# First mixture of experts: results scattered with addition into one zeroed array instead of copied into two

## Chip, cores and metric

One core of one Trainium2 chip runs the whole kernel. The metric is the device time in microseconds (us) of one execution. The other seven cores are not used.

## What is computed

The reference is a graph network with two layers on 6250 nodes of width 256 and 100000 edges. Each layer is an attention step over the graph followed by a mixture of experts, and each of the four steps is added to its own input x. Cut to what matters here, the first mixture is

```python
rh = relu(features @ router_w1 + router_b1)
top_w, top_i = top_k(softmax(rh @ router_w2 + router_b2), 2)
weights = softmax(top_w)
# three layers for each of 6 experts, width 256
out = sum over the two chosen experts e of weights[e] * expert_e(features)
x = x + out
```

and what follows it is the second layer's projection, `h = layernorm(x) @ W` with two attention scores for each node, from which the second attention gathers rows by edge.

So every node gets exactly two rows of results from the first mixture, from two different experts, and the second projection needs x plus both.

## The kernel before

Nodes are laid out in 49 tiles of 128 rows. x itself stays in on-chip memory as `x_all`. The kernel is written in stages, and inside each stage the order of the work on each engine is written out by hand (`manual_schedule`).

**ffn0** is the first mixture with the first attention woven in. Its loop runs once per pair of tiles and then on until everything has drained. One turn of the loop does, for different pairs, blocks and groups at once: gather neighbours' rows (`takes0`, on POOL's queue), mix them into x, normalise, score the experts, choose two, and give every chosen row a slot in the region of its expert. `scatters` (L768, tile `f_rows`) then writes the rows to their slots in memory, with one indirect DMA for each tile and choice. A full region gives a *block* of 256 rows of one expert. `fetch` reads a block back (`xr`, on SP's queue, with that expert's weights `w`), and PE runs the three layers (L1038 and L1048). `drawn` scales the result on ACT (`by`, L892), and `finish` adds the bias on DVE (L897). There are 54 blocks.

Each block's result goes out in two halves of 128 rows with `send`, an indirect DMA on POOL's queue (L903, tile `f_parts`), 108 of them in all. The target `parts` has two halves, one for first choices and one for second choices, so that no row is written twice. `places` works out the row for each result (`btok`, six buffers; DVE L878 to L880). All these writes are declared independent of each other, so none waits for another. Up to two blocks are done per turn, so up to four sends are queued per turn.

POOL's queue also carries the two gathers for each tile, the scatters, and 49 small writes (`meta_d`, L232) that belong to the later sorting of nodes by degree. A round-robin deals these lists onto the queue. Where two of a kind would follow each other, a tiny `gap` memset is put between:

```python
lists = [steps, results, dispatch[:k], extra]
while any(lists):
    for k, x in enumerate(lists):
        if x:
            ...
            x.pop(0)()
```

After the loop, `sources` puts 49 gathers of edge lists (`idx`, L253) on POOL's queue.

**gnn1** is the second projection. `load` brings four tiles of each half of `parts` at a time on SP's queue (tile `yg`, L1186). `begin` adds both to `x_all` on DVE (L1203, two additions for each pair of tiles). `projected` then runs a software pipeline over 25 pairs of tiles: moments on DVE (L397, L398), square root and normalisation on ACT (L478, L471), transposes on PE (L475), a copy on ACT (`xT`, L462), projection on PE (`proj`, L446), a copy on ACT (`hb`, L481), and two stores to the table `t_d` (L1211, L1212). When the table has landed, POOL starts the second attention's gathers (`own` L1229, `g` L1239).

Of the kernel before, what the change touches and what calls it, by code (L numbers as in the profile page):

```python
# [35 lines left out]
def gnn_moe_kernel(ctx: ExitStack, tc: tile.TileContext, a: dict, out: bass.AP):  # L36
# [587 lines left out]
    class Routed:  # L624
# [2 lines left out]

        def __init__(self, name, n_e, keep_pool, ids, own=False, spare=None):  # L630
            self.name, self.n_e, self.ids, self.own = name, n_e, ids, own
            self.n_blocks = (2 * N + n_e * (NB - 1)) // NB
            self.spare = spare
            self.planned = self.n_blocks if spare is None else (2 * N + spare) // NB
            self.null_row = n_e * REG

            self.round = 0
            self.written_by = []
            self.part = NT * P + self.n_blocks * NB
            self.parts = dram.tile([2 * self.part, D], F32, name=f"{name}_parts")  # L640
            self.table = dram.tile([n_e * REG + NB, RW], F32, name=f"{name}_rows")
            self.kp = kp = keep_pool
            rank = kp.tile([P, n_e], F32, name="rank")
            nc.gpsimd.iota(rank, pattern=[[-1, n_e]], base=n_e, channel_multiplier=0,
                           allow_small_or_imprecise_dtypes=True)
            reg = kp.tile([P, n_e], F32, name="reg")
            nc.gpsimd.iota(reg, pattern=[[REG, n_e]], base=0, channel_multiplier=0,
                           allow_small_or_imprecise_dtypes=True)
            eid = kp.tile([P, n_e], F32, name="eid")
            nc.gpsimd.iota(eid, pattern=[[1, n_e]], base=0, channel_multiplier=0,  # L650
                           allow_small_or_imprecise_dtypes=True)
            valid = kp.tile([P, 1], F32, name="valid")
# [214 lines left out]
        def places(self, pool, xr, bcol, j, tok=None):  # L867

            w = pool.tile([P, NTB], F32, name="bw", bufs=4)
            first = pool.tile([P, NTB], F32, name="bfirst", bufs=4)  # L870
            nc.vector.tensor_scalar(first, xr[:, :, C_E0], bcol[:, self.n_c : self.n_c + 1], None, op0=OP.is_equal)
            nc.vector.tensor_mul(w, xr[:, :, C_WD], first)
            nc.vector.tensor_add(w, w, xr[:, :, C_W1])
            if tok is None:
                tok = pool.tile([P, NTB], I32, name="btok", bufs=6)

            off = pool.tile([P, NTB], F32, name="boff", bufs=4)
            nc.vector.tensor_scalar(off, xr[:, :, C_TOK], float(NT * P), float(j * NB), op0=OP.is_ge, op1=OP.mult)  # L878
            nc.vector.tensor_add(off, off, xr[:, :, C_TOK])
            nc.vector.scalar_tensor_tensor(tok, first, float(self.part), off, op0=OP.mult, op1=OP.add)  # L880
            return w, tok, first

        def put(self, pool, b, i, py):


            y = self.drawn(pool, b, i, py)
            self.finish(b, i, y)
            return y, b["tok"][:, i : i + 1]

        def drawn(self, pool, b, i, py):  # L890
            y = pool.tile([P, D], F32, name="by", bufs=4 if self.own else 12)
# [7 lines left out]
                nc.vector.scalar_tensor_tensor(y, b["xr"][:, i, :D], b["first"][:, i : i + 1], y,  # L899
                                               op0=OP.mult, op1=OP.add)  # L900

        def send(self, y, tok):
            put = nc.gpsimd.indirect_dma_start(  # L903
                out=self.parts[:, :], out_offset=bass.IndirectOffsetOnAxis(ap=tok, axis=0),
                in_=y, in_offset=None,
            )
            self.apart(put, "parts")
            tc.add_to_no_dep_group(f"{self.name}parts", put.ins)

        def due(self, n_rows, last):  # L910

# [13 lines left out]
        def left(self, out_i):  # L925
# [5 lines left out]
            nc.vector.tensor_tensor(s[0:1, 1:2], s[0:1, 1:2], s[0:1, 0:1], OP.max)  # L931
            nc.vector.tensor_copy(out_i, s)


    def prepare0(fp, k):

# [10 lines left out]
        bcast_rows(bias_b, a["L1_gnn_bias"])  # L947
        k["we1"], ab1 = gat_load(k["g1w"], a["L1_gnn_W"], (a["L1_gnn_att_src"], a["L1_gnn_att_dst"]))
        yield None
        k["moe"] = moe = Routed("f0", NX, fp, w_row)  # L950
        yield None
        bc = fp.tile([P, NX, 4], F32, name="b12c")
        with tc.tile_pool(name="f0cp", bufs=1, space=PSUM) as psum:
# [8 lines left out]
    def ffn0(k0, t0_d, a0_d, late, order_pool):  # L962
        NX = a["L0_ffn_expert_w1"].shape[0]
        moe, rw1, rw2, rb1, rb2 = (k0[k] for k in ("moe", "rw1", "rw2", "rb1", "rb2"))
        with tc.tile_pool(name="f0g", bufs=1) as fp, tc.tile_pool(name="f0r", bufs=2) as rp, \
                tc.tile_pool(name="f0w", bufs=4) as wp, tc.tile_pool(name="f0h", bufs=2) as hp, \
                tc.tile_pool(name="g0b", bufs=2) as gp:
            with tc.tile_pool(name="f0p", bufs=2, space=PSUM) as psum:
# [102 lines left out]

                while s < len(pairs) or ready or coming or new or q1 or q2 or q3 or g1 or g2 or g3 or drawn \
                        or dispatch or late or metas:
                    cur, new = new, [fetch(*b) for b in ready[:2]]
                    ready = ready[2:]
                    for b, i, y in drawn:
                        moe.finish(b, i, y)
                        results.append(partial(moe.send, y, b["tok"][:, i : i + 1]))
                    drawn = []
                    chore()  # L1080
                    for b in cur:
# [54 lines left out]
                    k = 2 if done < moe.n_blocks else 6  # L1136
                    extra, metas = metas[:k], metas[k:]
                    k = 8
                    lists = [steps, results, dispatch[:k], extra]
                    dispatch = dispatch[k:]  # L1140
                    while any(lists):
                        for k, x in enumerate(lists):
                            if x:
                                if k == last_kind and k != 0:
                                    nc.gpsimd.memset(gap, 0.0)
                                x.pop(0)()
                                last_kind = k
                    results = []
                    if g2 is not None:
                        dispatch += moe.scatters(g2["n"], g2["rw"], g2["slot"], g2["last"])  # L1150
# [18 lines left out]
    def gnn1(moe0, we, bias_b):  # L1169
# [3 lines left out]
        with tc.tile_pool(name="g1", bufs=2) as pool, tc.tile_pool(name="g1p", bufs=2, space=PSUM) as psum:  # L1173
# [3 lines left out]
            def load():  # L1177
                if not loads:
                    return
                g, n = loads.pop(0)  # L1180
                for c in range(2):
                    y = pool.tile([P, 4, D], F32, name=f"yg{c}", bufs=4)
                    r = c * moe0.part + g * P
                    k = min(n, NFULL - g)
                    if k:
                        nc.sync.dma_start(y[:, :k, :], moe0.parts[r : r + k * P, :].rearrange("(t p) d -> p t d", p=P))  # L1186
                    if k < n:
                        nc.sync.dma_start(y[:NTAIL, k, :], moe0.parts[r + k * P : r + k * P + NTAIL, :])
                    ys[g, c] = y

            def begin(q):
                if q is None:
# [2 lines left out]
                o = g % 4  # L1195
                if o == 0:
                    load()
                for c in range(2):
                    y = ys[g - o, c]
                    k = min(n, NFULL - g)  # L1200
                    if k:
                        xs = x_all[:, g : g + k, :]
                        nc.vector.tensor_add(xs, xs, y[:, o : o + k, :])  # L1203
                    if k < n:
                        xs = x_all[:NTAIL, NFULL, :]
                        nc.vector.tensor_add(xs, xs, y[:NTAIL, o + k, :])

            def store(q, hb):
                g, n = q["g"], q["n"]
# [1 line left out]
                nc.sync.dma_start(tv[:, :, :CX], hb[:, :n, :])  # L1211
                nc.sync.dma_start(tv[:, :, CX:], x_all[:, g : g + n, :])  # L1212

            for _ in range(3):
                load()
            projected(pool, psum, we, begin, store, lambda: None, lambda: False)
        return tab
# [203 lines left out]
    def ffn1(tab, bias_b):  # L1421
        NX, _, HD = a["L1_ffn_W1"].shape
        NM = HD // P
        with tc.tile_pool(name="f1", bufs=1) as fp, tc.tile_pool(name="f1r", bufs=2) as rp, \
# [13 lines left out]
            with tc.tile_pool(name="f1p", bufs=2, space=PSUM) as psum:  # L1438
# [74 lines left out]
                def fetch_kept(j):  # L1513
                    y = hp.tile([P, NTB, D], F32, name="late", bufs=3)
                    nc.sync.dma_start(y, y_d[j * P : (j + 1) * P])
                    return [partial(moe.send, y[:, i, :], toks[:, j, i : i + 1]) for i in range(NTB)]

                gap = fp.tile([1, 1], F32, name="gap")
                s = 0
# [250 lines left out]
```

## Time and profile before

| | us |
|---|---|
| median of 3 runs | 2446.48 (2446.15 to 2448.04) |
| the profiled execution, its own time | 2447.71 |
| its span, first to last instruction | 2446.0 |
| PE busy, share of the span | 1848.9 (76%) |
| POOL busy | 1498.5 (61%) |
| DVE busy | 1222.0 (50%) |
| ACT busy | 943.2 (39%) |
| 108 sends of the first mixture (L903), busy on POOL | 105.5, 977 ns each |

By the trace, the first projection fills about the first 125 us, ffn0 runs to about 734 us, gnn1 from there to about 835 us, the second attention with the second mixture to about 2383 us, and the final sum and output to the end.

PE is TensorE, PEld its weight loads, DVE VectorE, ACT ScalarE, POOL GpSimd, and SP the engine that issues most direct DMAs. Issuing instructions on SP do not count as busy. In a timeline row the first number is the start in us, the second the duration, and the bracket at the end gives the idle time before it and what ended that. A "landing" is the time from an issue until its data are there.

### The profile page before, as it was taken

The numbers are of one execution on the slowest core, as the hardware profiler recorded it, in microseconds if no ns is written. First come the engines' busy times: TensorE is split into PE (matmuls) and PEld (weight loads), VectorE is DVE, ScalarE is ACT, GpSimd is POOL, SyncE is SP. The second block draws the span as 40 slices with busy tenths as digits, with TensorE's granted clock in tenths as the row PEclk, the third lists the DMA queues.
The fourth block names the chain that finished last, engine by engine and source line by source line (L and its number), as shares of the span: only waits on it lengthen the run. The fifth ranks groups of instructions, "written<-read, shape, count | busy, mean of one in ns | idle before, by whom it ended". The sixth has DMA issues, their size and how long they took to land.

```text
span 2446.0 us, 31094 instructions
## 1 busy us (share of the span) xinstructions
PE 1848.9 (76%) x8343; PEld 1545.0 (63%) x8344; DVE 1222.0 (50%) x4459; ACT 943.2 (39%) x1967; POOL 1498.5 (61%) x1778
## 2 busy tenths in 40 slices
PE   3834757887986455259699999999989797799990
PEld 2622546676774343247588888887778676588880
DVE  3658765653227545365555565655645454311112
ACT  2754445553445421014244444433433332334330
POOL 2556366767637377777777777777777774244420
PEclk8955778998998876679899999999999898899995
DMA  7513354768769644446667767676666665387748
GB/s 215 125 42 118 107 161 134 220 191 243 232 196 299 182 116 109 109 155 188 189 197 245 244 209 243 204 226 222 204 199 204 200 198 157 123 295 258 277 163 314
DMA packets 346251, 471.68 MB, mean 193 GB/s; under 512 B 70205, under 2 KB 283236, under 8 KB 346070
## 3 DMA queue, kind: packets, MB, share of 16 engines
q1 hardware_dynamic: 261868, 272.15, 35.6%
q0 software_dynamic: 72112, 186.44, 25.6%
q10 hardware_dynamic: 12090, 11.03, 1.3%
q8 instruction: 69, 1.13, 0.2%
q14 instruction: 112, 0.92, 0.1%
HBM read 374.44 MB, written 95.02 MB: 192 GB/s over the span
## 4 chain that ended last, share of the span: by engine, by line
PE 38%; POOL 16%; DMA 10%; issue 9%; DVE 7%; ACT 7%; SPq 1%; POOLq 0%; DVEq 0%; ACTq 0%
PE py L1481 10%; PE ph L1470 10%; POOL g L1239 10%; PE sums L1293 7%; PE ph L1038 5%; DMA g<-t_d,idx 4%; POOL f_rows L768 2%; PE py L1048 2%; POOL idx L253 2%; DMA yg<-f_parts 2%; DMA idx<-src_d,start_i 2%; DVE g L1284 1%; ACT L1474 1%; ACT L402 1%; POOL f_parts L903 1%
## 5 line engine op out<-in xcount | busy, mean ns | idle before, releaser
L1239 POOL DMA_INDIRECT g<-t_d,idx x813 | 776.7, 955 | 249.2 <-issue 229.5
L1470 PE MATMUL ph<-bxT,w 128*128 128x256 f32 x1728 | 411.7, 396 | 29.6 <-ACT hT L1474 29.6
L1470 PEld LDWEIGHTS ph<-bxT,w 128*128 128x128 f32 x1728 | 338.2, 199 | 90.5 <-ACT hT L1474 43.0
L1293 PE MATMUL sums<-g,ident 128*128 128x256 f32 x1626 | 386.5, 397 | 3.1 <-DVE g L1284 3.0
L1481 PE MATMUL py<-w,hT 128*128 128x256 f32 x1728 | 384.9, 381 | 0.3 <-DMA w<-in_L_ffn_W 0.3
L1293 PEld LDWEIGHTS sums<-g,ident 128*128 128x128 f32 x1626 | 323.1, 200 | 59.9 <-DVE g L1284 12.5
L1481 PEld LDWEIGHTS py<-w,hT 128*128 128x128 f32 x1728 | 328.3, 191 | 45.1 <-DMA w<-in_L_ffn_W 0.5
L768 POOL DMA_INDIRECT f_rows<-rw,slot x196 | 199.4, 1017 | 91.8 <-issue 45.9
L897 DVE SCALAR_TENSOR_TENSOR by<-ob,bw,by 128x256 f32<-128x256 f32 x216 | 98.0, 481 | 266.9 <-ACT by L892 266.9
L1474 ACT ACTIVATE hT<-ph,bcol 128x256 f32<-128x256 f32 x432 | 177.9, 472 | 137.5 <-PE ph L1470 132.2
L1284 DVE TENSOR_TENSOR g<-g,weights 128x2048 f32<-128x2048 f32 (+6 forms) x88 | 229.6, 2610 | 0.0
L903 POOL DMA_INDIRECT f_parts<-by,btok x108 | 105.5, 977 | 153.1 <-DVE by L897 105.3
L1263 ACT ACT_TABLE_LOAD x36 | 46.2, 1283 | 391.7 <-DVE lg L1262 268.3
L1550 PE MATMUL pT<-ident,xn 128*128 128x128 f32 x98 | 24.5, 341 | 184.8 <-DVE xn L1547 184.8
L892 ACT ACTIVATE by<-py,bw 128x256 f32<-128x256 f32 x216 | 92.5, 473 | 154.9 <-PE py L1481 121.8
L1041 ACT ACTIVATE h<-ph,bcol 128x256 f32<-128x256 f32 x216 | 90.7, 471 | 158.6 <-PE ph L1038 97.8
L903 POOL DMA_INDIRECT f_parts<-by,toks x44 | 42.3, 961 | 161.8 <-DVE by L899 123.2
L1550 PEld LDWEIGHTS pT<-ident,xn 128*128 128x128 f32 x98 | 13.4, 167 | 197.5 <-issue 188.7
L1254 DVE TENSOR_TENSOR lg<-g,own 128x32 f32<-128x32 f32 (+6 forms) x88 | 16.7, 199 | 238.3 <-DMA g<-t_d,idx 211.2
L446 PE MATMUL proj<-we,xT 128*128 128x264 f32 x392 | 107.7, 421 | 27.5 <-ACT xT L462 27.5
L1038 PE MATMUL ph<-bxT,w 128*128 128x256 f32 x432 | 110.6, 412 | 16.0 <-ACT bxT L864 14.9
L1038 PE MATMUL ph<-h,w 128*128 128x256 f32 x432 | 112.8, 420 | 0.6 <-ACT h L1041 0.6
(325 smaller groups left out, 2909.7 us busy)
## 6 DMA issues: line engine op xcount, KB each, us to landing
w<-in_L_ffn_W SPq DMA_DIRECT2D x108, 1024.0 KB
w<-in_L_ffn_expert_w SPq DMA_DIRECT2D x162, 256.0 KB
xr<-f_rows SPq DMA_DIRECT2D x108, 264.0 KB
yg<-f_parts SPq DMA_DIRECT2D x36, 512.0 KB
g<-t_d,idx POOLq DMA_INDIRECT x813, 3.2
late_y<-by SPq DMA_DIRECT2D x64, 128.0 KB
late<-late_y SPq DMA_DIRECT2D x32, 256.0 KB
ob<-in_L_ffn_expert_b SPq DMA_DIRECT2D x54, 128.0 KB
```

Source lines behind the costliest of these rows:

```text
L446: nc.tensor.matmul(ph, xT[:, k, :], we[:, k, :], start=(k == 0), stop=(k == 1))
L768: put = nc.gpsimd.indirect_dma_start(out=self.table[:, :], out_offset=bass.IndirectOffsetOnAxis(ap=slot[:np_, c, i : i + 1], axis=0), in_= ...
L892: nc.scalar.activation(y, py, AF.Copy, scale=b["w"][:, i : i + 1])
L897: nc.vector.scalar_tensor_tensor(y, b["ob"], w, y, op0=OP.mult, op1=OP.add)
L903: put = nc.gpsimd.indirect_dma_start(out=self.parts[:, :], out_offset=bass.IndirectOffsetOnAxis(ap=tok, axis=0), in_=y, in_offset=None,)
L1038: nc.tensor.matmul(ph[:, m, :], b["ws"][i][:, k, m * P : (m + 1) * P], hi[:, k, :], start=(k == 0), stop=(k == 1))
L1239: nc.gpsimd.indirect_dma_start(out=g[:, k, :], out_offset=None, in_=halves(tab), in_offset=bass.IndirectOffsetOnAxis(ap=idx[:, o : o + 1], ...
L1284: nc.vector.tensor_mul(gv, gv, al[:, k0 : k0 + m, :, None].to_broadcast([P, m, H, C]))
L1293: nc.tensor.matmul(po, ident, g[:, k, :D], start=False, stop=k0 + k == q["K"] - 1)
L1470: nc.tensor.matmul(ph[:, q, :], b["w1"][:, k, m * P : (m + 1) * P], b["xT"][:, k, :], start=(k == 0), stop=(k == 1))
L1474: nc.scalar.activation(hT[:, m, :], ph[:, q, :], AF.Gelu, bias=b["bcol"][:, m : m + 1])
L1481: nc.tensor.matmul(py, b["hT"][:, m, i * P : (i + 1) * P], b["w2"][:, m, :], start=(m == 0), stop=(m == NM - 1))
```

## The change

A new array `f0_sum` of one row per node takes the place of the two-halved `parts` for the first mixture. The second mixture, which has the same class, keeps `parts`.

- In the first seven turns of ffn0's loop, `clear` sets seven tiles each of the array to zero with one DMA on SP's queue, from a tile of zeros.
- Each `send` becomes an indirect DMA that adds its rows to the array. Rows that stand for padding have a number beyond the array and are dropped.
- Two sends of one block are declared independent. A send of another block is not, so it waits on POOL until the sends of the block before it have landed.
- `places` needs only a copy of the row number in place of three operations.
- In POOL's queue, only the first block's two sends stay in the round-robin. The second block's two sends go behind all else in the turn.
- gnn1 loads four tiles from one array (five buffers, four loads ahead, where there were four buffers for each half and three loads ahead) and does one addition for each pair, not two.

```diff
+            if result is None:
+                self.part = NT * P + self.n_blocks * NB
+                self.parts = dram.tile([2 * self.part, D], F32, name=f"{name}_parts")
 ...
+            if self.result is not None:
+                nc.vector.tensor_copy(tok, xr[:, :, C_TOK])
+                return w, tok, first
 ...
+        def send(self, y, tok, j):
+            if self.result is not None:
+                put = self.added(y, tok)
+                tc.declare_no_dep(put.ins, group=f"{self.name}sum{j}", reason="other rows")
+                tc.add_to_no_dep_group(f"{self.name}sum{j}", put.ins)
+                return
 ...
+        def added(self, y, tok):
+            return nc.gpsimd.indirect_dma_start(
+                out=self.result[:, :], out_offset=bass.IndirectOffsetOnAxis(ap=tok, axis=0),
+                in_=y, in_offset=None, bounds_check=self.result.shape[0] - 1, oob_is_err=False, compute_op=OP.add,
+            )
 ...
+    def clear(rows, zero, g, n):
+        k = min(n, rows.shape[0] // P - g)
+        nc.sync.dma_start(rows[g * P : (g + k) * P, :].rearrange("(t p) d -> p t d", p=P),
+                          zero[:, None, :].to_broadcast([P, k, D]))
 ...
+                    if s < NT // 7:
+                        clear(k0["sum"], moe.null[:, 0, :D], s * 7, 7)
 ...
-                    lists = [steps, results, dispatch[:k], extra]
+                    lists = [steps, results[:2], dispatch[:k], extra]
 ...
+                    for x in results[2:]:
+                        if last_kind == 1:
+                            nc.gpsimd.memset(gap, 0.0)
+                        x()
+                        last_kind = 1
 ...
-                for c in range(2):
-                    y = pool.tile([P, 4, D], F32, name=f"yg{c}", bufs=4)
 ...
+                y = pool.tile([P, 4, D], F32, name="yg", bufs=5)
+                nc.sync.dma_start(y[:, :n, :], moe0.result[g * P : (g + n) * P, :].rearrange("(t p) d -> p t d", p=P))
 ...
+                xs = x_all[:, g : g + n, :]
+                nc.vector.tensor_add(xs, xs, ys[g - o][:, o : o + n, :])
 ...
-            for _ in range(3):
+            for _ in range(4):
                 load()
```

More of the change, by code (lines that the diff above doesn't have):

```diff
@@ L624, in gnn_moe_kernel, with __init__ @@
     class Routed:
-        def __init__(self, name, n_e, keep_pool, ids, own=False, spare=None):
+        def __init__(self, name, n_e, keep_pool, ids, result=None, own=False, spare=None):
+            self.result = result
             self.name, self.n_e, self.ids, self.own = name, n_e, ids, own
@@ L638, in __init__ @@
             self.written_by = []
-            self.part = NT * P + self.n_blocks * NB
-            self.parts = dram.tile([2 * self.part, D], F32, name=f"{name}_parts")
+            if result is None:
+                self.part = NT * P + self.n_blocks * NB
+                self.parts = dram.tile([2 * self.part, D], F32, name=f"{name}_parts")
             self.table = dram.tile([n_e * REG + NB, RW], F32, name=f"{name}_rows")
@@ L887, in put @@
             self.finish(b, i, y)
-            return y, b["tok"][:, i : i + 1]
+            return y, b["tok"][:, i : i + 1], b["j"]
         def drawn(self, pool, b, i, py):
@@ L900, in finish @@
                                                op0=OP.mult, op1=OP.add)
-        def send(self, y, tok):
+        def send(self, y, tok, j):
[4 more added lines that the diff above has]
+                return
             put = nc.gpsimd.indirect_dma_start(
@@ L932, in left @@
             nc.vector.tensor_copy(out_i, s)
+    def clear(rows, zero, g, n):
+        k = min(n, rows.shape[0] // P - g)
+        nc.sync.dma_start(rows[g * P : (g + k) * P, :].rearrange("(t p) d -> p t d", p=P),
+                          zero[:, None, :].to_broadcast([P, k, D]))
+        if k < n:
+            nc.sync.dma_start(rows[NFULL * P : N, :], zero[:NTAIL, :])
     def prepare0(fp, k):
@@ L949, in prepare0 @@
         yield None
-        k["moe"] = moe = Routed("f0", NX, fp, w_row)
+        k["sum"] = dram.tile([NT * P, D], F32, name="f0_sum")
+        k["moe"] = moe = Routed("f0", NX, fp, w_row, k["sum"])
         yield None
@@ L1077, in ffn0 @@
                         moe.finish(b, i, y)
-                        results.append(partial(moe.send, y, b["tok"][:, i : i + 1]))
+                        results.append(partial(moe.send, y, b["tok"][:, i : i + 1], b["j"]))
                     drawn = []
@@ L1180, in load @@
                 g, n = loads.pop(0)
-                for c in range(2):
-                    y = pool.tile([P, 4, D], F32, name=f"yg{c}", bufs=4)
[L1183 to L1189, printed above, removed]
+                y = pool.tile([P, 4, D], F32, name="yg", bufs=5)
+                nc.sync.dma_start(y[:, :n, :], moe0.result[g * P : (g + n) * P, :].rearrange("(t p) d -> p t d", p=P))
+                ys[g] = y
             def begin(q):
@@ L1197, in begin @@
                     load()
[L1198 to L1206, printed above, removed]
+                xs = x_all[:, g : g + n, :]
+                nc.vector.tensor_add(xs, xs, ys[g - o][:, o : o + n, :])
             def store(q, hb):
@@ L1515, in fetch_kept @@
                     nc.sync.dma_start(y, y_d[j * P : (j + 1) * P])
-                    return [partial(moe.send, y[:, i, :], toks[:, j, i : i + 1]) for i in range(NTB)]
+                    return [partial(moe.send, y[:, i, :], toks[:, j, i : i + 1], j) for i in range(NTB)]
                 gap = fp.tile([1, 1], F32, name="gap")
```

## Prediction

> **What bounds the kernel now.** I read the page first for the shares, then the busy time by stretch, because the change touches two stages only: ffn0 (125 to 734 us) and gnn1 (734 to 835). Columns are busy time with instruction counts, then PE clock, DMA share and GB/s.
>
> ```profile
> 530.00:650.00 120.00, 99.01 (x478) 84.89 (x477) 43.36 (x221) 50.25 (x120) 94.47 (x126) 0.93 0.78 227
> 650.00:734.00 84.00, 75.34 (x360) 63.98 (x360) 24.63 (x106) 38.71 (x90) 30.92 (x59) 1.00 0.72 216
> 740.00:800.00 60.00, 42.03 (x187) 32.26 (x188) 47.57 (x138) 40.10 (x114) 46.16 (x64) 0.87 1.04 316
> ```
>
> From 530 to 650 POOL, the fifth column, is busy 94.5 of 120 us. Nearly every gap in it is the 0.30 us between two indirect DMAs, so its queue has no room. From 650 to 734 POOL has room and PE bounds (75 of 84). From 740 to 800 DVE is the busiest, at 47.6 of 60. The end of ffn0 on POOL's timeline:
>
> ```profile
> 721.93 0.96 POOL L903 DMA_INDIRECT f_parts<-by,btok  x1 [7.15 <-DVE by L897]
> ...
> 723.19 1.02 POOL L903 DMA_INDIRECT f_parts<-by,btok  x1 [0.22 <-issue]
> ...
> 724.51 0.96 POOL L903 DMA_INDIRECT f_parts<-by,btok  x1 [0.22 <-issue]
> ...
> 725.78 0.96 POOL L903 DMA_INDIRECT f_parts<-by,btok  x1 [0.22 <-issue]
> ...
> 732.28 0.96 POOL L903 DMA_INDIRECT f_parts<-by,btok  x1 [5.46 <-DVE by L897]
> ```
>
> Four sends follow each other 1.27 us apart without waiting, then POOL waits for PE's next blocks. How long a send takes to land, from the view of L903 in 530-600, 600-650, 650-700 and 700-735, in that order:
>
> ```profile
> DMA to landing us min/median/max: 3.1/5.0/6.4
> DMA to landing us min/median/max: 3.9/4.8/7.1
> DMA to landing us min/median/max: 5.2/5.5/7.0
> DMA to landing us min/median/max: 2.4/3.9/5.5
> ```
>
> Now this is hidden, since no send waits for another. Last, gnn1's pipeline, in the timeline from 756 us:
>
> ```profile
> 756.70 0.65 ACT L462 COPY xT<-ln_pT 128x256 f32<-128x256 f32 x2
> 757.13 2.05 PE L446 MATMUL proj<-we,xT 128*128 128x264 f32 x8 [0.31 <-ACT xT L462]
> 758.89 1.41 DVE L1203 TENSOR_TENSOR x_all<-x_all,yg 128x512 f32<-128x512 f32 x2
> 759.21 0.38 ACT L481 COPY hb<-proj 128x264 f32<-128x264 f32 x1 [0.37 <-PE proj L446]
> 759.49 0.65 ACT L462 COPY xT<-ln_pT 128x256 f32<-128x256 f32 x2
> ```
>
> **The change part by part.**
>
> *Waits between sends (added; decides).* Call a turn's sends A1, A2 (first block), B1, B2 (second). B1 now waits for A's landing, and the next turn's A1 for B's. All on POOL's queue behind a waiting send is held too: scatters `f_rows` (for which the fetch `xr` waits), meta writes, neighbour gathers (for which DVE waits). Once the six `btok` buffers are used, DVE, and through it PE, follows POOL's pace. Let L be the time from B2's or A2's start to the next block's first start, and a slot 1.265 us (0.96 busy plus 0.30). I walk the new queue from 530.85, where POOL had been idle 6.99 us and a turn starts on DVE's data:
>
> - Three turns with 8 scatters and 2 metas (old starts 530.85, 549.75, 567.53). B1 stands ten slots after A2, so it is covered. B2 is 13 slots (16.4 us) after A1, then comes L: 3 x (16.4 + L).
> - The turn at 586.34: A2 is 3 slots in (3.8), B1 waits L, B2 one slot (1.3), then B2's and 12 metas' slots cover the next A1 (16.4): 21.5 + L.
> - Two turns with 6 metas: 9 slots each, 11.4 + L, twice.
> - One turn with 1 meta (2.5 + L + 1.3 + L) and one with none (1.3 + L + 1.3 + L).
>
> The turn that began at 652.52 then begins at 530.85 + 49.2 + 21.5 + 22.8 + 3.8 + 2.6 + 10 L = 630.7 + 10 L. From there to the last turn (732.28) there are seven turns of two slots and two waits: 17.7 + 14 L, where before PE gave 79.8. The last A1 thus starts at 648.4 + 24 L. With one L throughout, ffn0 ends as before when L is 3.5; above, each further us costs 24.
>
> Which L? The rows give 5.0 for the ten waits up to 650, 5.5 for ten of the later ones, 3.9 for the last four, after the last fetches: 50 + 55 + 15.6 = 120.6, an end of 769.0, or +36.7 us. An adding send must also read its target, which no row shows. Lower bound for that extra r: 0 (hidden in the pipeline), or below nothing, if turns that take longer thin the traffic so that everything lands earlier: -0.5. Upper bound: 2 us. The nearest row is a gather of as many rows in quiet (L568, 120 to 150 us), 2.9 us for a whole trip against 2.4 for the quickest send, so a full trip more would be near the upper end. I take 0.5[...]: 24 x 0.5 = 12. **+48.7 us.**
>
> Here the Trainium skill speaks for the other sign. Its page "DMA: Bandwidth & Descriptors", section "Anatomy of one DMA — SWDGE (gpsimd) path", puts a DMA issued by GpSimd at about 2.0 us fixed plus bytes over 436e3. For 128 KB that is an estimate of 2.3 us; two waits and two slots then take 7.1 us where PE needs 11.4, so the chain is free and the sum is that of the first rival below, 2438, where the row gives 2488. The trace has 2.4 us only as the minimum in quiet; at a DMA share of 0.7 to 0.8 it has 4.8 to 5.5. I take the row. The 2 us above come from the same page ("Latency and other measured facts"): 0.2 us for a memory access on average, 2 at high load.
>
> *The same waits before 530 us.* In the turns from 301 to 355, 380 to 453 and 457 to 508 a wait has one or two gathers before it, so 2 to 3 us stay uncovered, but the second block's sends now stand behind the scatters, which come 2.5 us earlier. POOL then sits idle 24.84, 4.84 and 7.65 us, which absorbs most. Between 0 and 8; I take +2.
>
> *POOL time of one send.* 0.96 us now; the slowest on record is 1.40. 32 sends in the full stretch x 0.44 = 14 us at most, 0 at least; the adding form writes as many rows, so 0.
>
> *Zeroing (added).* Seven DMAs of 917 KB, 6.4 MB. SP has nothing to do then:
>
> ```profile
> 122.37 0.43 SPq L541 DMA_DIRECT2D a_d<-hb  x1
> 228.45 0.41 SPq L844 DMA_DIRECT2D xr<-f_rows  x1
> ```
>
> So all seven go out at about 123 us, before the first turns, and fill the DMA for some 20 us (6.4 MB at 316 GB/s). The first neighbour gathers start at 125.79, and DVE waits for them until 132.08. They land in 2.9 us in quiet; gathers beside a full DMA (L253, 735 to 798) take 6.0. So the first pair comes 3 us later; later ones run ahead of need. Between 0 and 5; **+3 us.**
>
> *places.* Three small DVE operations become one, 54 times. DVE is busy 340 of 609 us in this stage, and PE and POOL cover it: 0. Gone with that cover, it could gain 54 x 2 x 0.2 = 20 us of DVE time, of which no wait in the trace is made.
>
> *gnn1.* Each of 25 pairs loses one addition of 0.70 us on DVE, whose period is 3.32 us (starts of `proj` at 802.57, 805.88, 809.20). Next late is the loop ACT `xT` - PE `proj` - ACT `hb` in the rows above: 0.43 + 2.05 + 0.31 = 2.79. So not 0.70 but 0.52 per pair. The loop starts 2.2 us earlier (one load and one addition less for the first pair, one addition less for the second), runs its first intervals of 4.78 and 3.42 on a cold PE clock, and then 22 of 2.79: 746.7 + 69.6 = 816.3 for the last `proj`, 828.05 before. DMA share of 1.04 falls, since 6.4 MB less are loaded. POOL's 49 `idx` gathers take 62 us and end at 799 before, so they do not become the bound. **-11.8 us.** Bounds: 0 if stores then pace it, -17.5 for the whole addition.
>
> *Sum.* +48.7 + 2 + 3 - 11.8 = +41.9 against the profiled execution's own 2447.7 (span 2446.0): 2489.6. That execution lies 1.2 above the median, so 2488. All after gnn1 is unchanged and shifts as a whole.
>
> **The rivals.**
>
> *The adding sends land quickly (faster).* One mechanism: at L of 3.5 or less, PE stays the bound of ffn0's end, the wait is free, and only gnn1's gain and the zeroing remain: 3 - 11.8 = -9, or 2438; 2435 if zeroing hides too. The point of balance, with the other terms, is L = 3.8. For it: the median over all sends is 3.8 and the quiet minimum 2.4. Against it: where it counts the medians are 4.8 to 5.5 before anything is added.
>
> *Adding is dear.* r = 2 us: 24 x 2 = 48 instead of 12, +78, or 2524; with slower POOL instructions 14 more.
>
> *gnn1 gives nothing.* If stores pace it, +54, or 2500. Against it: DVE waited for loads only at the start (8.3 us), and the bytes fall.
>
> *It does not do what it says.* Would the waits not be there, the result were the first rival's. The built order shows them: a send of each new block waits on the previous block's DMA semaphore.
>
> **How the numbers follow.** The sends' chain as sized: 0.71, with 2464 (r of -0.5) to 2524. Dear adding beyond that: 0.06. Quick landing: 0.18. Balance within 0.2% (4.9 us, about what a measurement of this kernel can tell from no change): 0.05. So slower 0.77, same 0.05, faster 0.18. The range reaches down to 2438, the quick case with zeroing paid, and up to 2524.
>
> **What would show it.** POOL's timeline from 650 on: A1, A2 a slot apart, then an idle of 4 to 5 us ended by the DMA `f_sum`, then B1, B2, and again. Turns 13 to 14 us apart, where before they were 11.4. ffn0's last send near 780. PE busy in that stretch below 0.9 of it. gnn1's `proj` 2.8 us apart. I am wrong if POOL's idle before a send still ends on DVE `by`, if sends land under 3.8 us, if the first al/gt wait moves by far more than 3 us, or if gnn1 stays at 3.3.

## The result, and the profile after

The changed kernel takes 2559.28 us (median of 4 runs, 2552.97 to 2562.07), the kernel before 2446.32 (4 runs, 2444.06 to 2448.04) on the same chip: a ratio of 1.0465, interval 1.0445 to 1.0485, or 113 us slower. The prediction had 2488. The sign was right and the mechanism in part: sends that wait for landings do cost time. But the loss is 2.7 times the 41.9 us of the sum, and most of what is missing lies in terms that had been put at 0 and at 2 us. Eight of the runs told below met chips on which every kernel of this case, the one before too, takes 3245 to 3375 us, and on which the changed kernel is not slower; what is said of the loss rests on none of them.

The two traces can be set against each other stage by stage, since ffn0's sends, the first load of results (`yg`) and the first gather of the second attention (`own`) stand in both.

| stretch of the trace, us | before | after | difference |
|---|---|---|---|
| start to first send | 278.3 | 280.5 | +2.2 |
| first to last send (ffn0) | 455.2 | 572.9 | +117.7 |
| last send to first load of results | 2.6 | 2.9 | +0.3 |
| first load of results to first `own` gather (gnn1) | 98.8 | 86.5 | -12.3 |
| from there to the end | 1611.1 | 1615.9 | +4.8 |
| span | 2446.0 | 2558.7 | +112.7 |

So gnn1 gives what was predicted, and all of the loss is in ffn0. The busy time by stretch of the changed kernel, for the same three stretches of work that the prediction showed of the kernel before (sends 47 to 78, 79 to 108, and the middle of gnn1; columns PE, PEld, DVE, ACT, POOL busy, then PE clock, DMA share, GB/s):

```profile
577.00:752.00 175.00, 107.77 (x463) 90.74 (x463) 34.27 (x166) 49.19 (x115) 114.60 (x143) 0.80 0.69 163
752.00:853.40 101.40, 65.04 (x290) 54.79 (x288) 17.30 (x67) 31.60 (x73) 47.34 (x58) 0.84 0.58 130
860.00:920.00 60.00, 48.99 (x224) 37.72 (x225) 42.38 (x145) 47.01 (x135) 46.29 (x46) 0.90 0.85 256
```

In the first stretch no engine is full: POOL is busy 115 of 175 us where it was 94 of 120, and PE falls to 62%. In the second PE goes from 75 of 84 us to 65 of 101. These engines wait. Only in gnn1 does the picture improve: PE 49 of 60 us instead of 42, and a DMA share of 0.85 where it was 1.04.

POOL's timeline of the changed kernel in ffn0's end (start, duration, and in brackets the idle time before and what ended it; the tiny `gap` fills are left out):

```profile
736.66 1.70 POOL L924 DMA_INDIRECT f_sum<-by,btok  x1 [3.02 <-DVE by L902]
...
738.67 1.56 POOL L924 DMA_INDIRECT f_sum<-by,btok  x1 [0.26 <-issue]
...
746.38 1.55 POOL L924 DMA_INDIRECT f_sum<-by,btok  x1 [6.12 <-DVE btok L879]
...
748.24 1.55 POOL L924 DMA_INDIRECT f_sum<-by,btok  x1 [0.27 <-issue]
...
752.75 1.74 POOL L924 DMA_INDIRECT f_sum<-by,btok  x1 [2.92 <-DVE by L902]
```

Two sends follow each other, then POOL stands for 3 to 6 us until they have landed, then two more: the pattern that the prediction described. From the second send of a block to the first of the next (its L) these rows have 7.71 and 4.51 us. The bracket names DVE's `btok` or `by`, but DVE had itself just been released by such a landing (its row before 746.38 is at 745.74, idle 7.47 us until the DMA `f_sum`, and the two `by` come right behind such rows at 735.99 and 752.12): a wait for several semaphores is put down to the last. The waits from 278 to 855 us, after (columns: us in total, times, longest):

```profile
DVE btok L879 <- DMA f_sum<-by,btok: 171.9, 26, 18.2
...
PE pT L864 <- DMA xr<-f_rows: 80.5, 15, 16.4
POOL f_sum L924 <- DVE by L902: 69.6, 19, 15.9
```

Before, in the same stage, the three were

```profile
POOL f_parts L903 <- DVE by L897: 105.3, 14, 24.8
...
DVE btok L880 <- DMA f_parts<-by,btok: 22.0, 5, 8.6
...
PE pT L862 <- DMA xr<-f_rows: 21.2, 6, 9.3
```

DVE now waits 172 us for landings, and PE four times as long for rows of the table, since the scatters that write those rows stand behind the sends on POOL's queue. POOL's own wait for results shrank by only 36 us. The second thing that the trace shows was put at 0 in the prediction. The group of sends, first after and then before (count, busy us, mean ns of one, idle before it):

```profile
L924 POOL DMA_INDIRECT f_sum<-by,btok x108 | 173.7, 1608 | 205.4 <-DVE by L902 69.6
```

```profile
L903 POOL DMA_INDIRECT f_parts<-by,btok x108 | 105.5, 977 | 153.1 <-DVE by L897 105.3
```

An adding send holds POOL for 1.6 us instead of 1.0, 68 us more for the 108.

### The profile page after: what moved, and what is told of

Read it like the earlier page. It is cut to its first block, busy times and chain, and to the rows that moved or that the text cites. A ratio compares the mean times of both kernels' runs of the same rounds, so it can differ in the third digit from the quotient of the medians.

```text
span 2558.7 us, 31047 instructions
## 1 busy us (share of the span) xinstructions
PE 1870.8 (73%) x8343; PEld 1561.4 (61%) x8344; DVE 1187.0 (46%) x4326; ACT 944.6 (37%) x1967; POOL 1570.2 (61%) x1806
## 3 DMA queue, kind: packets, MB, share of 16 engines
q0 software_dynamic: 82480, 185.10, 27.2%
## 4 chain that ended last, share of the span: by engine, by line
PE 28%; POOL 15%; DMA 7%; issue 7%; ACT 5%; DVE 4%; SPq 0%; POOLq 0%; DVEq 0%; ACTq 0%
POOL g L1261 10%; PE py L1503 10%; PE ph L1492 10%; PE sums L1315 7%; DMA g<-t_d,idx 3%; POOL idx L253 2%; POOL f_rows L770 2%; DMA yg<-f_parts 2%; ACT L1496 1%; DMA idx<-src_d,start_i 1%; DVE g L1306 1%; ACT L402 1%; ACT hT L1496 1%; ACT bxn L1511 1%; ACT L1285 1%
## 5 line engine op out<-in xcount | busy, mean ns | idle before, releaser
L1492 PE MATMUL ph<-bxT,w 128*128 128x256 f32 x1728 | 409.0, 394 | 28.9 <-ACT hT L1496 28.9
L1492 PEld LDWEIGHTS ph<-bxT,w 128*128 128x128 f32 x1728 | 336.3, 198 | 88.8 <-ACT hT L1496 42.4
L924 POOL DMA_INDIRECT f_sum<-by,btok x108 | 173.7, 1608 | 205.4 <-DVE by L902 69.6
L1066 PE MATMUL ph<-bxT,w 128*128 128x256 f32 x432 | 124.3, 450 | 10.0 <-ACT bxT L866 8.8
L1066 PEld LDWEIGHTS ph<-bxT,w 128*128 128x128 f32 x432 | 98.1, 234 | 30.7 <-ACT bxT L866 11.6
```

Source lines behind the costliest of these rows:

```text
L924: return nc.gpsimd.indirect_dma_start(out=self.result[:, :], out_offset=bass.IndirectOffsetOnAxis(ap=tok, axis=0), in_=y, in_offset=None, ...
L1066: nc.tensor.matmul(ph[:, m, :], b["ws"][i][:, k, m * P : (m + 1) * P], hi[:, k, :], start=(k == 0), stop=(k == 1))
L1492: nc.tensor.matmul(ph[:, q, :], b["w1"][:, k, m * P : (m + 1) * P], b["xT"][:, k, :], start=(k == 0), stop=(k == 1))
```

## Experiments

Three theories of the loss were set against each other. The first is the prediction's: the chain of landings carries it. The second is the price of the adding form, POOL's time above all. The third is the six `btok` buffers: DVE may not write new row numbers before an old send has landed, and so carries the wait into routing. The parts of the change were then done one by one, all but the shorter `places`. Differences in time below are the ratio's distance from 1 times the median of the kernel before that was measured beside it, with its interval. "Mixture" is the time from the first to the last send in the trace, 455.2 us before; it is split at send 47 (530.85 us before), where the prediction's walk began.

**Waits alone.** Sends of the kernel before, copying into two arrays, but ordered and grouped as in the changed kernel:

```diff
-            tc.add_to_no_dep_group(f"{self.name}parts", put.ins)
+            k = "parts" if self.own else f"parts{j}"
+            tc.add_to_no_dep_group(f"{self.name}{k}", put.ins)
...
-                    lists = [steps, results, dispatch[:k], extra]
+                    lists = [steps, results[:2], dispatch[:k], extra]
```

> The kernel before (copying sends, two arrays, no zeroing) in which the sends of a block wait until the sends of the block before have landed, and stand in the order of the changed kernel. The theory of the waits (the chain of landings carries the loss): 55 us or more slower than before, 2505 to 2525. The theory that the price of an adding send carries it: at most 20 us slower, 2450 to 2465.

Measured: 2502.09, ratio 1.0228 (1.0205 to 1.0252), so 56 us slower (50 to 62). The mixture grows by 60.6 us, 12.8 of them before send 47 and 47.8 after it. The waits, with the order of the sends that goes with them, are thus about half of the loss, and they cost it with copies. Its waits show the same two rows as the changed kernel, smaller:

```profile
DVE btok L880 <- DMA f_parts<-by,btok: 119.1, 21, 16.3
...
PE pT L862 <- DMA xr<-f_rows: 56.7, 12, 14.2
```

**Adding alone.** Sends that add, each to its own row of the two arrays, both set to zero first, no waits:

```diff
-                in_=y, in_offset=None,
+                in_=y, in_offset=None, **({} if self.own else dict(compute_op=OP.add)),
...
+                    if s < NT // 7:
+                        for c in range(2):
+                            clear(moe.parts[c * moe.part : ...], moe.null[:, 0, :D], s * 7, 7)
```

> The kernel before with sends that add into its two arrays, both set to zero first, without any wait between sends. The theory of the waits: near before, 2450 to 2465. The theory that the price of an adding send carries the loss (108 sends at 1.57 us of GpSimd's time and not 0.96 are 66 us): 2500 or more.

Measured: 2491.58, ratio 1.0199 (1.0173 to 1.0225), 49 us slower (42 to 55). The theory of the waits expected 2450 to 2465 and fails here; neither theory alone holds. The group of sends on the page:

```profile
L903 POOL DMA_INDIRECT f_parts<-by,btok x108 | 172.2, 1594 | 122.5 <-DVE by L897 74.7
```

and the median time from issue to landing (last column), first of before, then of this kernel:

```profile
f_parts<-by,btok POOLq DMA_INDIRECT x108, 4.9
```

```profile
f_parts<-by,btok POOLq DMA_INDIRECT x108, 6.3
```

So the adding form has two prices, POOL's 0.6 us and a landing 1.4 us later; no run shows how much of the 1.4 is the longer instruction itself. In the mixture it costs 18.1 us before send 47 and 16.7 after, together 34.8. The 49 us of the whole also hold the zeroing of two arrays, and the profiled execution was the quickest of its four (2484). Once the routing is done (from send 73 on) it costs nothing: the lag is 34.5 us there and 35.0 at the end, since PE bounds that stretch and no send waits for another.

**More buffers for the row numbers.** The changed kernel with `btok` of 12 buffers instead of 6 (and `bfirst` of 2 instead of 4, to make room).

> The changed kernel with 12 buffers and not 6 for the row numbers of the sends (two and not four for bfirst, to make room), so that VectorE no longer waits for sends of the turn before to land before it may write the next numbers. The theory that this wait on VectorE carries the landings into the routing and the next turn: 40 us or more faster than the changed kernel, 2500 to 2525. The theory that GpSimd's own chain of landings carries it: 0 to 15 us faster, 2545 to 2560.

Measured: 2561.41, ratio 1.0476 (1.0453 to 1.05), not faster than the changed kernel's 1.0465 (1.0445 to 1.0485). As it was stated, the third theory falls. DVE's wait of 172 us for `btok` is gone from the trace, and three other rows have taken its place. The second and third are waits for the same landings, and the first hands the second on to DVE:

```profile
DVE by L902 <- ACT by L897: 150.1, 44, 12.6
...
ACT by L897 <- DMA f_sum<-by,btok: 57.7, 21, 9.2
...
POOL f_sum L924 <- DMA f_sum<-by,btok: 38.1, 9, 6.3
```

The longest row of a table of waits need not be the one that costs. But a wait for buffers in general is not excluded: `by` has 12 buffers of half a block, as many blocks as six of `btok`, and DVE now waits for it. More buffers of both were not tried.

**No check of bounds.** The changed kernel drops padding rows by a bound. Here they get rows of their own behind the tokens:

```diff
-                in_=y, in_offset=None, bounds_check=self.result.shape[0] - 1, oob_is_err=False, compute_op=OP.add,
+                in_=y, in_offset=None, compute_op=OP.add,
```

> The changed kernel with sends that check no bounds: the padding slots of a block go to rows of their own behind the tokens, so every one of the 256 rows of a send is moved and added. If the longer time of a send on GpSimd (1.57 us in the changed kernel, 0.96 before) comes from the adding form, the row stays at 1.5 to 1.6 us and the time within 15 us of the changed kernel. If it came from checking the bounds of an addition, the row falls to about 0.96 us, and the theory that this price carries the loss expects 50 us or more less than the changed kernel; the theory of the waits alone expects 10 to 25 us less.

Measured: 2564.43, ratio 1.0488 (1.0458 to 1.0518), as the changed kernel. A send stays at a median of 1578 ns (second of the three numbers), so the longer time is the adding form's:

```profile
L924 POOL DMA_INDIRECT f_sum<-by,btok x108: 1552/1578/2775, 280.3 to 854.5; - x108
```

One thing differs, the last turns. From a block's second send to the next block's first, most of the last waits take 3.4 to 3.5 us in the changed kernel (848.10 to 851.58 is the last) and 4.4 to 4.6 here. The padding rows are the likely reason: this kernel's software queue moves 186.44 MB where the changed kernel's moves 185.10.

**The second projection alone.** The kernel before, but gnn1 loads one array and makes one addition; the other half's results are left out.

> The kernel before with only the second projection changed as the edit changes it: it loads one array of results and makes one addition for a token tile (the other half's results are left out). Every theory of the loss expects the projection's part alone: 10 to 12 us faster than before, 2434 to 2437. If this gain does not reach the end, it is within 5 us.

Measured: 2432.46, ratio 0.9944 (0.9926 to 0.9962), 14 us faster (9 to 18). The loop has the predicted period of 2.79 us (3.32 before):

```profile
795.45 2.05 PE L446 MATMUL proj<-we,xT 128*128 128x264 f32 x8 [0.31 <-ACT xT L462]
...
798.24 2.05 PE L446 MATMUL proj<-we,xT 128*128 128x264 f32 x8 [0.31 <-ACT xT L462]
```

**Zeroing alone.** The kernel before with the seven zeroing transfers into an array that nothing reads.

> The kernel before with the seven zeroing transfers of the changed kernel, into an array that nothing reads. The prediction's term: 3 us slower, 0 to 5. If zeroing delayed the first rows' loads or the weights, more than 5.

Measured: 2449.01, ratio 1.0019 (1.0008 to 1.003), 4.6 us slower (2.0 to 7.3). The predicted 3 lies in it.

**POOL's time alone.** To part the adding form's two prices, POOL is kept busy after each copying send by a fill of 620 elements in memory that is not in use then:

```diff
             tc.add_to_no_dep_group(f"{self.name}parts", put.ins)
+            if not self.own:
+                nc.gpsimd.memset(idx[:1, :620], 0)
```

> The kernel before, with copying sends and no waits, in which GpSimd fills memory for about 0.6 us after each of the 108 sends, as long as an adding send takes more than a copying one. If GpSimd's time is what the adding form costs: 35 to 50 us slower than before, like the run with adding sends and no waits (2491). If its transfers are what costs: within 10 us of before.

Measured: 2471.51, ratio 1.0107 (1.009 to 1.0124), 26 us slower (22 to 30). POOL's timeline shows that the fill has the right length, 0.60 us:

```profile
639.63 0.96 POOL L903 DMA_INDIRECT f_parts<-by,btok  x1 [0.30 <-issue]
640.59 0.62 POOL L910 MEMSET idx<- 1x620 int32 x1
641.39 0.96 POOL L232 DMA_INDIRECT meta_d<-meta,rank_i  x1 [0.17 <-issue]
642.66 0.96 POOL L903 DMA_INDIRECT f_parts<-by,btok  x1 [0.30 <-issue]
```

It falls between the two expectations. In the mixture it costs 13.3 us before send 47 and 9.9 after. So about two thirds of what the adding form costs the mixture without waits is POOL's time (23 of 35 us), the rest the transfers.

**POOL's time and waits.** The same fill in the kernel with waits.

> The same 0.6 us of GpSimd after each copying send, in the kernel whose blocks wait for each other. If the 23 us that no single part explains are GpSimd's time standing in the chain of landings: 115 to 130 us slower than before, which is the changed kernel without its projection's gain of 12. If the two costs only add: 95 to 105 slower. If the adding transfers themselves carry the rest: at most 95.

Measured: 2529.11, ratio 1.0356 (1.0332 to 1.0381), 87 us slower (81 to 93), less than the 95 to 105 that were expected of a plain sum, since that counted the whole price of adding. The fill's 26 and the waits' 56 simply add, to 82. So POOL's time behind a send is not what makes the changed kernel dearer than its parts, and about 40 us were still missing. Two limits of the fill: it stands for most of the adding form's time but not all (from a block's first send to its second 1.77 us with the fill, 1.86 with adding sends, 1.26 with copies alone), and it comes behind the send, so it cannot show what a longer send does to its own landing.

**Waits and adding, in two arrays.** Everything that the mixture of the changed kernel has but the one array, the bound and the short `places`. In its gnn1, which lies behind the mixture and is read separately, another way to spare DVE an addition is tried: from the third group of tiles on, the second half is added to the first by the transfer that loads it, issued by POOL.

```diff
+                    into = c if g < 8 else 0
...
+                    q, how = (nc.sync, {}) if c == into else (nc.gpsimd, dict(accum_op=OP.add))
```

> Mixture: waits, order and adding sends as in the changed kernel, but into two zeroed arrays. Projection: the second half added by the transfer that loads it, the first two groups as before. Each is read from its own stretch. From the first send to the last (before 455, changed 573, waits and busy time 541): about 573 if the adding transfers carry the 40 us, about 541 if one array, the check of bounds or the table loads do. From the first load of results to the first gather of the next layer (before 98.8, changed 86.5): 87 to 93 if adding loads keep the pace, 98 or more if they are too slow. Whole, if both hold: 105 to 120 us slower than before.

Measured for the mixture: 576.5 us from first to last send, against 572.9 in the changed kernel and 539.7 with waits and busy time. So it is the adding sends themselves, when they are waited for, that carry what was missing, and not the one array or the check of bounds. They land later; whether the transfer or POOL's longer instruction in front of it makes them late was not parted. What a wait costs can be read where little else runs, in the last turns. The rows are a block's second send and the next block's first, with copies (waits and busy time) and then with adding (this kernel):

```profile
808.87 0.96 POOL L903 DMA_INDIRECT f_parts<-by,btok  x1 [1.54 <-issue]
...
810.64 0.97 POOL L903 DMA_INDIRECT f_parts<-by,btok  x1 [0.17 <-issue]
...
813.82 0.96 POOL L903 DMA_INDIRECT f_parts<-by,btok  x1 [1.57 <-DMA f_parts<-by,btok]
```

```profile
852.22 1.55 POOL L903 DMA_INDIRECT f_parts<-by,btok  x1 [2.96 <-issue]
...
854.08 1.55 POOL L903 DMA_INDIRECT f_parts<-by,btok  x1 [0.26 <-issue]
...
858.65 1.55 POOL L903 DMA_INDIRECT f_parts<-by,btok  x1 [2.98 <-DMA f_parts<-by,btok]
```

From 810.64 to 813.82 is 3.18 us, from 854.08 to 858.65 it is 4.57: counted from its start, an adding send is done 1.4 us later.

Its gnn1 is a miss. From the first load to the first gather it takes 114.5 us (864.3 to 978.8), where before has 98.8. The adding loads land 10.8 us after their issue (last column, on POOL's queue), and DVE's additions, 2.75 us apart in the first two rows below, then come at gaps of 6.5 and 4.9:

```profile
yg<-f_parts POOLq DMA_DIRECT2D x10, 512.0 KB, 10.8
```

```profile
892.47 0.69 DVE L1225 TENSOR_TENSOR x_all<-x_all,yg 128x512 f32<-128x512 f32 x1
...
895.22 0.68 DVE L1225 TENSOR_TENSOR x_all<-x_all,yg 128x512 f32<-128x512 f32 x1
...
901.73 0.69 DVE L1225 TENSOR_TENSOR x_all<-x_all,yg 128x512 f32<-128x512 f32 x1
...
906.67 0.68 DVE L1225 TENSOR_TENSOR x_all<-x_all,yg 128x512 f32<-128x512 f32 x1
```

The whole kernel takes 2592.15, ratio 1.06 (1.0579 to 1.0621), 147 us slower (142 to 152): the mixture's 121, its first send 5.6 later with twice the zeroing, and a gnn1 that loses 16.

**Adding by load, first version.** The same idea in the kernel before, for all groups of tiles, with three of POOL's edge-list gathers ahead of each adding load (one ahead of the first).

> The kernel before with copying sends into two arrays, in which the second half is added to the first by the transfer that loads it (queued by GpSimd between its gathers of the list of edges), so that VectorE has one addition for a token tile. If VectorE's two additions are what sets the projection's pace and the adding loads come in time: 5 to 12 us faster than before. If an adding load lands too late, or takes GpSimd longer than its gathers leave: same or slower, up to 20.

Measured: 2456.58, ratio 1.0045 (1.0028 to 1.0062), 11 us slower (7 to 15). The first adding load was issued at 737.31 and DVE's first addition came at 746.52, after a wait of 17.47 us. So on chips like the first no version here beats the kernel before with the whole result computed, and neither form of the adding load reaches the 14 us of the single addition.

**The runs on the other chips.** Five repeat kernels above: the waits alone had a ratio of 0.9993, adding alone 0.9765, 12 buffers 0.9966, gnn1 alone 0.9957, and the second version of adding by load, whose gnn1 is that of the last but one experiment, 0.9957. Three more had no other run, or were the changed kernel itself. The order alone (the sends' places in POOL's queue as changed, without the waits):

> The kernel before with the queue order alone: the second block's two sends go behind all else in the turn, without waits. Both theories: within 5 us of 2446, since these sends still land long before their buffers are needed.

Measured: 1.0001 (0.999 to 1.0012). The changed kernel:

> The changed kernel itself, unaltered, beside the kernel before, to have both on the same chip as the kernels that undo one part. If its ratio is that of the first measurement (1.0445 to 1.0485), the parts can be set against it directly. If it is nearer to 1, the loss depends on what else holds up the mixture: every theory here (waits for landings, price of an adding send, table buffers) puts the loss on the path of GpSimd and VectorE through the mixture, so it would be covered where those engines are held up by something else.

Measured: 0.9894 (0.9866 to 0.9921). The mixture with waits and adding in two arrays, with the old gnn1:

> The kernel before with the waits and the order of the changed kernel and with sends that add, but into two zeroed arrays, with both read by the old projection. If the adding transfers themselves carry what is left: 115 to 130 us slower than before (2560 to 2575). If one array, the check of bounds or the loads of the table carry it: near the kernel with waits and busy time, 80 to 95 slower.

Measured: 0.9951 (0.993 to 0.9971). There the sign of the result turns: the changed kernel is about 1% faster, and adding alone 2.3%. From first to last send, kernels with copying sends take 585.0 us (order alone), 601.4 (gnn1 alone) and 595.4 (adding by load); beside them on the same chips, adding alone takes 505.7, the changed kernel 570.0, waits and adding 579.8. That the loss would only be covered, as the second case of the expectation for the changed kernel has it, does not explain a gain, and why adding sends shorten the mixture there is open. What the order alone costs on a chip like the first was not measured either; it is part of the waits' 56 us here.

## Why the prediction was wrong in size

The mixture from the first to the last send, split at the start of the prediction's walk:

| kernel | to send 47 | from send 47 | together |
|---|---|---|---|
| before | 252.5 | 202.7 | 455.2 |
| waits and order | +12.8 | +47.8 | +60.6 |
| waits and busy POOL | +31.5 | +53.0 | +84.5 |
| waits and adding, two arrays | +42.8 | +78.6 | +121.3 |
| changed | +44.7 | +73.0 | +117.7 |

Read downwards, the waits with their order cost 61 us, POOL's longer time 24 more, and the later landing of adding sends 37 more. Since the fill stands for 0.51 of 0.60 us, an estimated 4 of the 37 belong to POOL's time.

*Waits between sends, from 530 us.* Predicted 48.7: 36.7 at the L of the rows, plus 12 for the read of the target (r = 0.5). The changed kernel lost 73.0. The waits with copies measured 47.8, so the walk was 11 short, though L itself was about right: the mean of the last 17 waits is 5.07 us with copies, where it took 5.5 for ten and 3.9 for four. POOL's longer time adds 5. What is left is r, and it was mis-sized: over 24 waits, 20.0 us or 0.83 each in the changed kernel, and 25.6 us or 1.07 each with two arrays. It is not one number either. In the last turns it is 1.4 us where every row is added, and 0.3 in most of the changed kernel's. The bounds given (-0.5 to 2) held it, but the nearest row named there, a full trip for a gather of as many rows, pointed to the upper end, and 0.5 was taken against it.

*The same waits before 530 us.* Predicted +2, since POOL's idle times there absorb "most". This is the largest miss: 44.7. With two arrays, where the parts were measured, it is 42.8, of which the waits are 12.8, POOL's time 18.7 and the landings 11.3. POOL's idle time that ends on DVE's `by` did shrink up to send 47, from 56.8 to 35.4 us, but the stage came later all the same, so it was not slack. The traces show it as the latency of a loop: a late send holds back the gathers and scatters behind it on POOL's queue, DVE waits for the gathers (`al`, 0.5 us before, 19.0 after), the routing comes later, PE waits for its rows (`rw`), and a later block delays the next send. The waits that grew, all of them before send 47, first of before (whose `al` row has 0.5 us), then of the changed kernel:

```profile
PE pT L1018 <- ACT rw L1010: 34.1, 13, 5.3
```

```profile
PE pT L1046 <- ACT rw L1038: 50.8, 13, 10.8
...
DVE s L581 <- DMA al<-a_d,src_i: 19.0, 5, 6.5
```

The rows read back from the table matter later: of PE's 80 us for `xr`, 69 come after send 47. The row-number buffers play no part before send 47: 164 of DVE's 172 us for `btok` come after it, and with 12 buffers this stretch takes 297.9 us against 297.2. The way round the loop is read from the waits; no experiment cut it at one place.

*POOL time of one send.* Predicted 0, at most 14 us. Alone it is 26 (22 to 30), with a fill that is a little short. The bound failed twice: 0.6 us and not 0.44, and counted for 32 sends, although half of the cost lies before 530 us, where the prediction took POOL to have room.

*Zeroing and `places`.* Predicted 3 and 0. Zeroing measured 4.6 (2.0 to 7.3). The first send came 2.2 us later, which alone would say little, since without zeroing it comes between 274.5 and 278.3 us in these runs. For `places`, no experiment did it alone; the kernel that keeps the old one (waits and adding, two arrays) has a mixture 3.6 us longer, which also holds its double zeroing.

*gnn1.* Predicted -11.8; the trace has -12.3, and alone it is -14 (-18 to -9). The period of 2.79 us that the rows of ACT and PE gave was exact.

*All after gnn1.* Predicted unchanged. It is 4.8 us longer. In the other runs with a chip like the first, which have no edit to this stretch either, it lies between 1609 and 1615 us, so most of that can be scatter.

*The Trainium skill's rule.* "DMA: Bandwidth & Descriptors", section "Anatomy of one DMA — SWDGE (gpsimd) path", gave an estimate of 2.3 us for a send of 128 KB and with it a faster kernel. The prediction set it aside for the trace's rows, rightly: with copies the chain has 3.2 us from one block's send to the next even in the quiet last turns and 5.07 on average over the last 17, so L fell below the balance of 3.8 only where the traffic had ended. The median of 3.8 us that the prediction held in favour of quick landing was of all sends on that line, the second mixture's too; the 108 of the first have 4.9.

*The chances.* Slower had 0.77, and slower it was, but beyond the range's upper end of 2524. The rival "adding is dear", r = 2 with slower instructions on POOL, gave 2538 and came nearest; it was given 0.06. It named the adding form's two prices, but it too left out the loss before 530 us.

## What to carry to other kernels

When an operation takes another form (a write that becomes an addition), its price on the issuing engine and its time to landing are both unknown until measured: let the range reach to the upper bound, and take the nearest row at its word. Before idle time is called slack, follow what ends it: if the wait is for something that the delayed instruction itself feeds, the idle time can move along and absorb little. And do the parts of a change one by one, then two at a time; here the parts alone would have left 22 us unexplained, and taking away the longest row in the table of waits gained nothing.

## What was not expected of the hardware

- A scatter of 128 rows by POOL takes 0.96 us as a copy and 1.55 to 1.6 as an addition, with or without a check of bounds. In the changed kernel a tiny fill behind it, 0.09 us otherwise, takes 0.61, but the two records overlap (a send at 730.18 of 1.56 us, its fill at 731.17): it is the same 0.6 us, shown twice.
- The adding sends bring 10368 more packets, 96 for each send, on the software queue. Before, then adding alone:

```profile
q0 software_dynamic: 72112, 186.44, 25.6%
```

```profile
q0 software_dynamic: 82480, 186.44, 27.5%
```

- In quiet, an adding send of all its rows frees the next one 1.4 us later than a copying one (4.57 us against 3.18).
- A load of 512 KB that adds to its target took 1.4 us of POOL and a median of 10.8 us to land, and with it gnn1 took 114.5 us instead of 98.8.
